# A two-layer scan network on one core: the second layer's side work cut into lagged units, its decays moved to SBUF, half of its scan sources multiplied by VectorE

## The chip, the cores and the metric

The kernel runs on one core of a Trainium2 chip. Five engines work from their own in-order queues: TensorE (PE, with its weight loads as PEld), VectorE (DVE), ScalarE (ACT), GpSimd (POOL) and SyncE (SP), which issues nearly all DMAs. The metric is the device time of one execution in microseconds, the median of several.

## The reference, cut to what matters

Batch 2, 2048 tokens, width 256, all in float32. Layer 0 (a small state-space block and a mixture of experts) is left as it is. Layer 1, which is changed, is a bidirectional Mamba block with a feed-forward part and a second branch:

```
for d in (fw, bw):                       # bw runs over time backwards
    xi, z = split(LN(x) @ Win);  u = silu(conv4(xi))
    dt, B, C = ...u @ Wx...;     dt = softplus(dt @ Wdt + bdt)
    h[t] = exp(dt*A) * h[t-1] + (dt*u) * B[t]        # 512 channels x 16 states
    y = sum_n h[.., n] * C[n] + u * D
    out_d = (y * silu(z)) @ Wout
f  = LN(x + out_fw) + LN(x + out_bw)     # scaled and shifted
f  = LN(f + relu(f @ W1 + b1) @ W2 + b2) # feed-forward part
out = x1 + f + gelu(LN(x) @ Wup + bup) @ Wdn + ...   # butterfly matrices, folded to dense
```

## The kernel before, in words

Layer 1 works in 16 chunks ("steps" in the code): for each of two batches four forward chunks of 512 tokens, then four backward ones. A chunk has 512 channels (four groups `e` of 128 partitions) and 16 states `n`, so 64 scans of 128 x 512. The loop over `g` at L1100 goes through all 1024 scans of the layer; `k` is the scan's place in its chunk.

Half of the scans are of kind P, half of kind D (`kinds`, L755: the first eight scans of a chunk are D, then P and D alternate, and the last eight are P).

- A P scan: ACT writes the decay `exp(dt*A)` to SBUF (`a`, L806), four scans ahead. ACT scales the transposed `dt*u` by B (`bT`, L792), PE transposes it back into a PSUM bank (`ab`, L816), DVE scans `h<-a,ab` (L836), POOL copies the last column (`hn`, L844) and multiplies `h` by C (`g`, L845).
- A D scan: ACT writes the decay into a PSUM bank of the same ring `ab`, one scan ahead. POOL multiplies `dtu` by the broadcast row of B (`b`, L823), DVE scans in place in the bank, ACT copies the last column (L847), DVE multiplies by C (L848).

The ring `ab` has two banks, which decays of D scans and sources of P scans take in turn. Four scans later `collect` (L850) lets PE transpose each `g` into four accumulators `yacc` (L870). At a chunk's first scan it opens them with a matmul of zeros (L859) and adds the skip term (L863).

All other work of a chunk is a list of functions with guessed weights (`prepare_parts`, `finish_parts`, `ff_parts`, `late_parts`) that is popped between the scans, in proportion to `k`, as whole functions: `down` issues all 32 of its matmul records, `project_out` adds, takes statistics, waits for POOL's root and normalizes, at one place of the program. A forward chunk has only the projections of its neighbours beside its scans; a backward chunk has in addition the whole feed-forward part and the second branch for both of its halves. The tile framework's own scheduler may then reorder what stands in one engine's queue. Side work uses a second ring of two PSUM banks, `pp`.

`delta_u` (L733) makes `dtu` for the next chunk on POOL; `skip_term` (L748) scales `u` there.

Of the kernel before, what the change touches and what calls it, by code (L numbers as in the profile page):

```python
# [18 lines left out]
P = 128  # L19
B = 2  # L20
# [9 lines left out]
class Common:  # L30
# [36 lines left out]
    def stats(self, pool, src, n):  # L67

        nc = self.nc
        bs = pool.tile([P, n, 6], F32, tag="bs", name="bs", bufs=2)  # L70
        mv = pool.tile([P, n, 2], F32, tag="mv", name="mv", bufs=2)
        rs = pool.tile([P, n], F32, tag="rs", name="rs", bufs=2)
        for i in range(n):
            nc.vector.bn_stats(bs[:, i, :], src[:, i, :])
            nc.vector.bn_aggr(mv[:, i, :], bs[:, i, :])  # L75
        self.rstd(rs, mv[:, :, 1])
        return mv, rs
# [413 lines left out]
TB = T // P  # L491
NT = L // T


def layer1(tc, c, a, x1d, wupd, wdnd, bupd, out):
    nc = c.nc
    with ExitStack() as ctx:
# [9 lines left out]


# [5 lines left out]
        def prologue(b, k):  # L514
            xnT = ap.tile([P, 2, T], F32, tag="xnT", name="xnT", bufs=3)
            for h in range(2):
                r = 2 * k + h
                x1t = tp.tile([P, 2, D], F32, tag="x1t", name="x1t", bufs=2)
                nc.sync.dma_start(x1t, rows2(x1d[b], r))
                mv, rs = c.stats(tp, x1t, 2)  # L520
                xn = tp.tile([P, 2, D], F32, tag="xn", name="xn", bufs=2)
                c.normalize(xn, x1t, mv, rs, 2)
                nc.sync.dma_start(rows2(xn1d[b], r), xn)
                ps = c.pp()
                for kk in range(2):
                    for i in range(2):
                        nc.tensor.transpose(
                            ps[:, kk * 256 + i * P : kk * 256 + (i + 1) * P],
                            xn[:, i, kk * P : (kk + 1) * P],
                            c.ident,  # L530
                        )
                nc.scalar.copy(
                    xnT[:, :, h * 256 : (h + 1) * 256], ps.rearrange("p (k t) -> p k t", k=2)
                )
            nc.sync.dma_start(xnTd[b][k], xnT)
            return xnT
# [39 lines left out]
        zero = wp.tile([P, P], F32, name="zero")  # L576
        nc.gpsimd.memset(zero, 0.0)
        ident4 = c.ident.unsqueeze(1).broadcast_to([P, 4, P])
# [68 lines left out]
        def gate(ck, zs, tb):  # L647

            ps = c.pp()
            for k in range(2):  # L650
                nc.tensor.matmul(
                    ps, ck.xnT[:, k, tb * P : (tb + 1) * P], ck.w["winz"][:, k, :],
                    start=(k == 0), stop=(k == 1),
                )
            nc.scalar.copy(zs[:, tb, :], ps)

        def conv(i, e):
# [5 lines left out]
            ps = c.pp()  # L663
            for k in range(2):
                nc.tensor.matmul(
                    ps, w["winx"][:, k, e * P : (e + 1) * P], ck.xnT[:, k, :],
                    start=(k == 0), stop=(k == 1),
                )
# [11 lines left out]
            for k in range(3):  # L680
                o = 3 - k if bw else k
                nc.vector.scalar_tensor_tensor(  # L682
                    ck.u[:, e] if k == 2 else ps, xi[:, o : o + T], pk[:, e, k : k + 1], ps,
                    ALU.mult, ALU.add,
                )
# [5 lines left out]

        def project(i):
            ck = steps[i]
            ps = c.pp()
            for e in range(4):
                nc.tensor.matmul(  # L696
                    ps, ck.w["wx"][:, e, :], ck.u[:, e, :], start=(e == 0), stop=(e == 3)
                )
# [5 lines left out]
        def rowsB(i):  # L704
            ck = steps[i]
            ps = c.pp()
            for tb in range(TB):
                nc.tensor.transpose(
                    ps[:, tb * P : (tb + 1) * P], ck.par[:, tb * P : (tb + 1) * P], c.ident
                )  # L710
            ck.BT = ap.tile([P, TB, NS], F32, tag="BT", name="BT")
            nc.scalar.copy(ck.BT, ps.rearrange("p (b m) -> p b m", b=TB)[:, :, 32:48])

        def delta(i, e):
# [6 lines left out]
            )  # L721
            nc.scalar.activation(
# [3 lines left out]
        def softplus(i):  # L726
            nc.scalar.activation(steps[i].dt, steps[i].dt, AF.Softplus)

        def delta_u(i, e):
# [3 lines left out]
            nc.gpsimd.tensor_mul(ck.dtu[:, e], ck.dt[:, e], ck.u[:, e])  # L733

        def delta_uT(i, tb):
# [8 lines left out]
            nc.scalar.copy(ck.dtuT[:, tb, :], ps)  # L744
# [10 lines left out]
        kinds = ["DD"] + ["PD"] * 6 + ["PP"]  # L755
# [9 lines left out]
        lo, hi = 0, 8  # L765
        for n in range(NS):
            ks = [k for k in range(K) if plan[k][1] == n and plan[k][3] == "P"]
            if ks:
                for q in range(TB):
                    fills[lo + q * (hi - lo) // TB].append((n, q))  # L770
                lo, hi = ks[0], ks[-1] + 1
# [25 lines left out]
        def decay(g):  # L797
            i, k = divmod(g, K)
            ck = steps[i]
            m, n, e, kind = plan[k]  # L800
            r = R[g] = {}
            if kind == "P":
                r["a"] = sp.tile([P, T], F32, tag="a", name="a", bufs=5)
            else:
                r["a"] = r["ps"] = c.ab()
            nc.scalar.activation(r["a"], ck.dt[:, e], AF.Exp, scale=ck.w["A"][:, e, n : n + 1])  # L806

        def source(g):
# [3 lines left out]
            r = R[g]  # L812
            if kind == "P":
                r["b"] = r["ps"] = c.ab()
                for q in range(TB):
                    nc.tensor.transpose(  # L816
                        r["b"][:, q * P : (q + 1) * P],
                        ck.bT[n, q][:, e * P : (e + 1) * P],
                        c.ident,
                    )  # L820
            else:
                r["b"] = sp.tile([P, T], F32, tag="b", name="b", bufs=3)
                nc.gpsimd.tensor_mul(r["b"], ck.dtu[:, e], ck.bb[n])  # L823

        def scan(g):
# [6 lines left out]
            if kind == "P":  # L832
                h = sp.tile([P, T], F32, tag="h", name="h", bufs=4)
            else:
                h = r["ps"]
# [5 lines left out]
            gt = r["g"] = sp.tile([P, T], F32, tag="g", name="g", bufs=6)  # L841
            hn = ck.hn[:, e, n : n + 1]
            if kind == "P":
                nc.gpsimd.tensor_copy(hn, h[:, last : last + 1])  # L844
                nc.gpsimd.tensor_mul(gt, h, ck.cb[n])  # L845
            else:
                nc.scalar.copy(hn, h[:, last : last + 1])  # L847
                nc.vector.tensor_mul(gt, h, ck.cb[n])  # L848

        def collect(g):  # L850
# [3 lines left out]
            if k == 0:  # L854
# [3 lines left out]
                for tb in range(TB):  # L858
                    nc.tensor.matmul(  # L859
                        ck.y[tb], zero, ident4, start=True, stop=False, skip_group_check=True  # L860
                    )
                    for e2 in range(4):
                        nc.tensor.matmul(  # L863
                            ck.y[tb][:, e2 * P : (e2 + 1) * P],
                            ck.u[:, e2, tb * P : (tb + 1) * P], c.ident,
                            start=False, stop=False, is_transpose=True, skip_group_check=True,
                        )
            gt = R.pop(g)["g"]
            for tb in range(TB):
                nc.tensor.matmul(  # L870
                    ck.y[tb][:, e * P : (e + 1) * P], gt[:, tb * P : (tb + 1) * P], c.ident,
                    start=False, stop=(k == K - 1), is_transpose=True, skip_group_check=True,
# [9 lines left out]
        def turned(i, e):  # L882
# [8 lines left out]
            nc.scalar.copy(ck.ygT[:, e, :], ps)  # L891
# [4 lines left out]
        def project_out(i, h):  # L896
# [3 lines left out]
            xn = tp.tile([P, 2, D], F32, tag="xn", name="xn", bufs=2)  # L900
            nc.sync.dma_start(xn, rows2(xn1d[ck.b], r))
            if ck.bw:
                yf = tp.tile([P, 2, D], F32, tag="yf", name="yf", bufs=2)
                nc.sync.dma_start(yf, rows2(yfd[ck.b][ck.k], h))
            ps = c.pp()
            for n in range(2):
# [336 lines left out]
```

## Time and profile before

| | us |
|---|---|
| median of 3 runs | 4137.5 (4127.43 to 4138.06) |
| the profiled execution, its own time | 4139.88 |
| its span, first to last instruction | 4138.2 |
| first scan of layer 1 starts | 1647.0 |
| last scan of layer 1 starts | 4045.4 |
| a forward chunk in the middle (first `gated` to the next, 1913.0 to 2046.1) | 133.1 |
| a backward chunk (2496.2 to 2677.2) | 180.9 |
| mean granted TensorE clock, as a share | 0.794 |

Times in the profile are microseconds from the first instruction; "mean" is in nanoseconds. L836 is line 836 of the kernel before. `out<-in` names the tiles. A group's idle time is how long its engine stood still just before the instructions of the group, with what ended the wait. A DVE or POOL instruction's own duration can contain a wait, where it has started and is held: such time counts as busy.

### The profile page before, as it was taken

How to read it: one execution, taken by the hardware profiler on the slowest of the kernel's cores; microseconds unless marked ns; L12 is line 12 of the kernel's file. 1: busy time of each engine (PE TensorE's matmuls, PEld its weight loads, DVE VectorE, ACT ScalarE, POOL GpSimd, SP SyncE). 2: the span in 40 equal slices, each digit the busy share in tenths (PEclk: the TensorE clock that was granted, in tenths of full speed). 3: DMA queues.
4: the chain of work that ended last, by engine and by line, in shares of the span. 5: the costliest groups of instructions: out<-in, count | busy, mean ns of one | idle time of the engine just before them, and what ended most of it. 6: DMA issues, size and time to landing. Idle time of an engine off the chain costs nothing.

```text
span 4138.2 us, 41758 instructions
## 1 busy us (share of the span) xinstructions
PE 2927.6 (71%) x13136; PEld 2056.6 (50%) x13136; DVE 3327.6 (80%) x4436; ACT 2353.4 (57%) x4721; POOL 2038.9 (49%) x2197
## 2 busy tenths in 40 slices
PE   6445364657677666777777778787877778888887
PEld 3323242434444433455555656575655555656565
DVE  7899999887988975888888767777788888767782
ACT  3433434354655654766766665655666766665662
POOL 5465555200000002677776656655577776656661
PEclk8657565657676676888889989898988888889898
DMA  4322142312122124312212121212121212111110
GB/s 135 119 96 67 59 125 102 100 44 76 32 66 67 34 59 128 101 60 66 61 60 75 59 73 46 78 56 69 52 67 60 63 65 70 54 52 52 47 46 13
DMA packets 170995, 285.07 MB, mean 69 GB/s; under 512 B 18571, under 2 KB 90443, under 8 KB 165644
## 3 DMA queue, kind: packets, MB, share of 16 engines
q1 hardware_dynamic: 170166, 280.30, 22.7%
q8 instruction: 104, 1.70, 0.2%
q0 software_dynamic: 608, 2.10, 0.1%
q14 instruction: 117, 0.96, 0.1%
HBM read 240.66 MB, written 24.91 MB: 64 GB/s over the span
## 4 chain that ended last, share of the span: by engine, by line
DVE 21%; PE 16%; POOL 9%; ACT 8%; issue 6%; DMA 0%; DVEq 0%; SPq 0%; POOLq 0%; ACTq 0%
DVE h L836 6%; DVE ab L836 6%; POOL g L845 3%; DVE g L848 3%; PE pp L962 3%; PE yacc L870 2%; POOL b L823 2%; PE ab L816 2%; ACT ab L806 2%; PE pp L696 2%; DVE pp L682 2%; PE pp L909 1%; POOL dtu L733 1%; ACT zu L690 1%; PE pp L1007 1%
## 5 line engine op out<-in xcount | busy, mean ns | idle before, releaser
L823 POOL TENSOR_TENSOR b<-dtu,bb 128x512 f32<-128x512 f32 x512 | 651.8, 1278 | 280.1 <-DVE ab L836 262.6
L427 PE MATMUL yacc<-da,ident 128*128 128x256 f32 x1024 | 449.9, 585 | 475.5 <-DVE da L424 410.2
L870 PE MATMUL yacc<-ident,g 128*128 128x128 f32 x4096 | 676.4, 302 | 144.2 <-POOL g L845 104.4
L870 PEld LDWEIGHTS yacc<-ident,g 128*128 128x128 f32 x4096 | 534.7, 156 | 264.4 <-POOL g L845 144.9
L845 POOL TENSOR_TENSOR g<-h,cb 128x512 f32<-128x512 f32 x512 | 651.8, 1273 | 0.4 <-POOL hc L844 0.2
L836 DVE TENSOR_TENSOR_SCAN h<-a,hc,ab 128x512 f32<-128x512 f32 x384 | 483.4, 1268 | 164.4 <-PE ab L816 155.1
L427 PEld LDWEIGHTS yacc<-da,ident 128*128 128x128 f32 x1024 | 268.5, 286 | 638.7 <-ACT hc L421 168.9
L816 PE MATMUL ab<-ident,bT 128*128 128x128 f32 x2048 | 373.1, 308 | 261.3 <-DVE h L836 168.5
L836 DVE TENSOR_TENSOR_SCAN ab<-ab,hc,b 128x512 f32<-128x512 f32 x384 | 485.5, 1277 | 70.7 <-ACT ab L806 68.0
L806 ACT ACTIVATE ab<-dt,A 128x512 f32<-128x512 f32 x512 | 351.5, 690 | 222.5 <-DVE h L836 113.0
L816 PEld LDWEIGHTS ab<-ident,bT 128*128 128x128 f32 x2048 | 264.9, 156 | 415.5 <-DVE h L836 243.2
L806 ACT ACTIVATE a<-dt,A 128x512 f32<-128x512 f32 x512 | 365.9, 717 | 160.5 <-DVE h L836 160.3
L417 DVE TENSOR_TENSOR_SCAN h<-da,h,bt 128x256 f32<-128x256 f32 x512 | 437.3, 891 | 8.9 <-ACT h L415 7.4
L64 POOL TENSOR_SCALAR rs<-mv 128x2 f32<-128x2 f32 (+1 forms) x72 | 16.6, 231 | 827.0 <-DVE mv L75 823.8
L401 ACT ACTIVATE da<-dt,A 128x256 f32<-128x256 f32 x512 | 235.1, 500 | 271.7 <-PE yacc L427 271.1
L848 DVE TENSOR_TENSOR g<-ab,cb 128x512 f32<-128x512 f32 x512 | 341.3, 678 | 55.3 <-ACT hc L847 54.9
L792 ACT ACTIVATE bT<-dtuT,BT 128x512 f32<-128x512 f32 x512 | 359.9, 717 | 10.5 <-PE ab L816 10.4
L405 DVE SCALAR_TENSOR_TENSOR bt<-dt,small,bt 128x256 f32<-128x256 f32 x512 | 333.3, 658 | 11.0 <-ACT bt L402 10.1
L844 POOL COPY hc<-h 128x1 f32<-128x1 f32 x512 | 103.1, 201 | 450.0 <-DVE h L836 407.6
L107 POOL TENSOR_TENSOR bft<-bfy,bfw 128x512 f32<-128x512 f32 (+1 forms) x100 | 158.6, 1604 | 321.9 <-DMA bfw<-in_upc_dram 165.9
L402 ACT ACTIVATE bt<-da,nc,c 128x256 f32<-128x256 f32 x512 | 280.6, 589 | 0.0
L847 ACT COPY hc<-ab 128x1 f32<-128x1 f32 x512 | 80.1, 157 | 253.4 <-DVE ab L836 251.1
(201 smaller groups left out, 5634.5 us busy)
## 6 DMA issues: line engine op xcount, KB each, us to landing
cb<-bcd SPq DMA_DIRECT2D x256, 256.0 KB
cb<-cd SPq DMA_DIRECT2D x128, 256.0 KB
bb<-bcd SPq DMA_DIRECT2D x128, 256.0 KB
bfw<-in_upc_dram SPq DMA_DIRECT2D x20, 1024.0 KB
bfw<-in_dnc_dram SPq DMA_DIRECT2D x20, 1024.0 KB
relay<-inter SPq DMA_DIRECT2D x128, 128.0 KB
f1c<-in_f_dram SPq DMA_DIRECT2D x8, 1024.0 KB
f2bd<-in_f_dram SPq DMA_DIRECT2D x16, 512.0 KB
```

The costliest lines, as they stand in the source:

```text
L402: nc.scalar.activation(bt[:, j], da[:, j], AF.Identity, scale=c1[:, e, s], bias=nc1[:, e, s])
L405: nc.vector.scalar_tensor_tensor(bt[:, j], dt[:, e], small[:, e, s], bt[:, j], ALU.mult, ALU.add)
L417: nc.vector.tensor_tensor_scan(h[:, j, 1 : LC + 1], da[:, j], bt[:, j], h[:, j, 0:1], ALU.mult, ALU.add,)
L427: nc.tensor.matmul(ys[e][:, 0:LC], c.ident, da[:, j], start=(n == 0), stop=(n == NS - 1))
L792: nc.scalar.activation(t, ck.dtuT[:, q, :], AF.Copy, scale=ck.BT[:, q, n : n + 1])
L806: nc.scalar.activation(r["a"], ck.dt[:, e], AF.Exp, scale=ck.w["A"][:, e, n : n + 1])
L816: nc.tensor.transpose(r["b"][:, q * P : (q + 1) * P], ck.bT[n, q][:, e * P : (e + 1) * P], c.ident,)
L823: nc.gpsimd.tensor_mul(r["b"], ck.dtu[:, e], ck.bb[n])
L836: nc.vector.tensor_tensor_scan(h[:, step], r["a"][:, step], r["b"][:, step], 0.0 if ck.first else steps[i - 1].hn[:, e, n : n + 1], ALU.mu ...
L845: nc.gpsimd.tensor_mul(gt, h, ck.cb[n])
L848: nc.vector.tensor_mul(gt, h, ck.cb[n])
L870: nc.tensor.matmul(ck.y[tb][:, e * P : (e + 1) * P], gt[:, tb * P : (tb + 1) * P], c.ident, start=False, stop=(k == K - 1), is_transpose=T ...
```

## The change

Only layer 1 changes (and `stats`, which is split into `moments` and the root).

1. **Scans.** All decays go to SBUF, six scans ahead (`AHEAD`, eight buffers instead of five). A D scan's source is multiplied by DVE straight into the `ab` bank that it then scans, so that PE (P) and DVE (D) alone write that ring. All scans write `h` to SBUF; POOL takes the last column and the multiply by C for all 64 (it had both for 32, and the source of the other 32). `collect` follows three scans later instead of four, and `g` has five buffers instead of six.
2. **Accumulators.** The zero matmuls go; the first transpose opens the bank, and the skip term is added later (`skip_term`, `skip_add`).
3. **Side work as units.** Each function is cut into units `U` of about two matmuls, each with followers that come a set number of scans later (`EV`, `DV`, `PO`, `PE`): a PE unit, then its copy out by ACT, then DVE, then the root on POOL, then DVE. `merged` interleaves several lists with at most two open `pp` banks, and `spread` stretches them over the chunk's scans. SiLU, softplus and GELU have fixed places (`SILU`, `SOFT`, `GELU`).
4. **Where the feed-forward work goes.** The second branch (`network_parts`) runs one half in every chunk, forward chunks too, and leaves `x1p` in DRAM. The rest (`ff_parts`) follows a chunk or more later (`FEEDS`), and reads `yd` and `x1p` back from DRAM.
5. **Moves between engines.** `delta_u` from POOL to DVE; two adds (`shift`, `last`) from DVE to POOL; the copies of the last column of D scans from ACT to POOL.
6. **Order.** Inside `tc.manual_schedule` the four compute engines keep the order in which the program is written. The prologue's `xnT` is read back from DRAM.

The core of the diff:

```diff
-        kinds = ["DD"] + ["PD"] * 6 + ["PP"]
+        kinds = ["DD", "PD", "PD", "PD", "PD", "PD", "PD", "PP"]
...
-            if kind == "P":
-                r["a"] = sp.tile([P, T], F32, tag="a", name="a", bufs=5)
-            else:
-                r["a"] = r["ps"] = c.ab()
+            assert ck.dt_made
+            r["a"] = sp.tile([P, T], F32, tag="a", name="a", bufs=AHEAD + 2)
             nc.scalar.activation(r["a"], ck.dt[:, e], AF.Exp, scale=ck.w["A"][:, e, n : n + 1])
...
-            else:
-                r["b"] = sp.tile([P, T], F32, tag="b", name="b", bufs=3)
-                nc.gpsimd.tensor_mul(r["b"], ck.dtu[:, e], ck.bb[n])
...
+            if kind == "D":
+                r["b"] = c.ab()
+                nc.vector.tensor_mul(r["b"], ck.dtu[:, e], ck.bb[n])
+            h = sp.tile([P, T], F32, tag="h", name="h", bufs=4)
             nc.vector.tensor_tensor_scan(
...
-            if kind == "P":
-                nc.gpsimd.tensor_copy(hn, h[:, last : last + 1])
-                nc.gpsimd.tensor_mul(gt, h, ck.cb[n])
-            else:
-                nc.scalar.copy(hn, h[:, last : last + 1])
-                nc.vector.tensor_mul(gt, h, ck.cb[n])
+            gt = r["g"] = sp.tile([P, T], F32, tag="g", name="g", bufs=5)
+            nc.gpsimd.tensor_copy(ck.hn[:, e, n : n + 1], h[:, last : last + 1])
+            nc.gpsimd.tensor_mul(gt, h, ck.cb[n])
...
-                for tb in range(TB):
-                    nc.tensor.matmul(
-                        ck.y[tb], zero, ident4, start=True, stop=False, skip_group_check=True
-                    )
...
-            nc.gpsimd.tensor_mul(ck.dtu[:, e], ck.dt[:, e], ck.u[:, e])
+            nc.vector.tensor_mul(ck.dtu[:, e], ck.dt[:, e], ck.u[:, e])
...
+EV, DV, PO, PE, LAG = 1.2, 1.2, 0.6, 1.2, 1.5
+AHEAD = 6
+FF_AT = 22
+BEHIND = 3
+LATE = 56
+SILU, SOFT, GELU = 32, 48, 14
...
+            us[3].then, us[3].closes = ((DV, norm), (PO, root), (DV, store), (PO, shift)), 0
...
+        with tc.manual_schedule(engines={nc.tensor.engine, nc.scalar.engine, nc.vector.engine, nc.gpsimd.engine}):
+            for g in range(-AHEAD, N + BEHIND):
+                if 0 <= g < N:
+                    i, k = divmod(g, K)
+                    if k == 0:
+                        todo = merged([early_parts(i)], 0, 1.0)[1]
+                        todo += spread(chains(i), BEHIND + 1.2, K - 0.5)
+                        todo.sort(key=lambda x: x[0])
+                    if k % 8 == 0 and k + 8 < K:
+                        load_bc(i, k // 8 + 1)
+                if 0 <= g + AHEAD < N:
+                    decay(g + AHEAD)
+                if 0 <= g < N:
+                    for n, q in fills[k]:
+                        scaled(i, n, q)
+                if 0 <= g + 1 < N:
+                    source(g + 1)
+                if 0 <= g < N:
+                    scan(g)
+                if 0 <= g - BEHIND < N:
+                    collect(g - BEHIND)
+                if 0 <= g < N:
+                    while todo and (todo[0][0] < k + 1 or k == K - 1):
+                        todo.pop(0)[2]()
```

## The prediction

> **What bounds the kernel now.** I read the page's engine totals first (DVE 80%), then the windows of layer 1, because an 80% over the whole span says nothing of the stage that is changed. The columns after the length are PE, PEld, DVE, ACT and POOL busy, the granted clock, and DMA:
>
> ```profile
> 1647.00:4047.00 2400.00, 1893.13 (x9723) 1391.72 (x9721) 1894.22 (x2232) 1565.90 (x2771) 1578.31 (x1914) 0.89 0.21 63
> 1904.00:2037.00 133.00, 101.79 (x524) 71.58 (x524) 113.44 (x127) 90.08 (x161) 95.04 (x117) 0.86 0.22 67
> 2487.00:2668.00 181.00, 146.63 (x734) 110.35 (x732) 129.35 (x164) 110.96 (x194) 105.27 (x130) 0.91 0.22 64
> ```
>
> The scans of layer 1 take 2400 us, 150.0 per chunk: 133 in a forward chunk, 181 in a backward one. DVE is busy for 118.4 of the 150 (1894.22/16), and in no chunk is any engine full. So the layer is paced by hand-overs. Who holds DVE up, from the waits of that stretch (total, times, longest):
>
> ```profile
> DVE h L836 <- PE ab L816: 202.2, 130, 9.1
> DVE ab L836 <- ACT ab L806: 89.5, 118, 4.9
> DVE g L848 <- ACT hc L847: 54.9, 131, 1.9
> DVE xn L82 <- POOL rs L65: 49.2, 40, 1.8
> DVE x1t L966 <- PE pp L962: 32.2, 12, 3.0
> DVE yf L82 <- POOL rs L65: 25.2, 14, 2.4
> ```
>
> P scans wait for their transposes, D scans for a decay that comes only one scan ahead, the multiply by C for ACT's copy, normalizing for POOL's root. Why the transposes are late is in PE's timeline of a backward chunk (start, duration):
>
> ```profile
> 2357.79 7.17 PE L962 MATMUL pp<-wdn,gff 128*128 128x256 f32 x32 [1.11 <-ACT hc L847]
> 2364.80 0.60 PE L816 MATMUL ab<-ident,bT 128*128 128x128 f32 x4
> ```
>
> One block of side work holds PE's queue for 7.2 us, and the sources of the next scans stand behind it. The same rows give PE's true pace: (7.17-0.4)/31 = 0.22 us per 256-column record, (0.60-0.27)/3 = 0.11 per transpose.
>
> **The change part by part**, per chunk of 64 scans. Consecutive instructions overlap a little, so I use start-to-start times where the timeline has them: a multiply on DVE 0.60 (two L880 take 1.26), a scan 1.19, a multiply on POOL 1.22 (four L733 take 4.95), its column copy 0.14.
>
> *DVE.* A D scan loses its multiply by C (678 ns, L848) and gains its source; the nearest row with two SBUF inputs is L919 at 683 ns, so nothing. The output in PSUM is bounded by L848 from PSUM and L682 at 736: at most 2 us, below nothing by the 8 ns to L1015 (670), taken as 0. delta_u comes in, 4 x 0.60 = +2.4; two adds per chunk leave, -1.2. DVE: 119.6.
>
> *POOL.* 98.6 now (1578.31/16). Less 32 sources (39.0) and 4 delta_u (4.9), plus 32 multiplies by C with copies (43.5), plus two adds (2.4): 100.6.
>
> *ACT.* 97.9 now, less 32 copies of 157 ns: 93. The table switches stay in number; SiLU with two loads is 1.28+3.62+1.28 = 6.2 us, which today stalls D scans whose decay is one ahead. Six decays ahead are some 12 us: hidden. Without that cover it would be up to 4 us at each of three places.
>
> *PE.* The zero matmuls go (83.8 us busy in all, off the path except at a chunk's head, where they wait for L880). What stays, by counts over 16: about 440 transposes x 0.11, 128 records of 256 columns x 0.22, 48 of 512 x 0.43 = 97 us at full clock, 109 at 0.89. It hides beside DVE, but at 84% of a 130 us chunk, not loosely: units of about 0.9 us between 0.44 us transposes.
>
> *The price that today's scans don't pay.* Every DVE instruction of the scan loop has one SBUF tensor and one in PSUM, and L836 never exceeds 1294 ns beside a busy POOL. The new source multiply reads two SBUF tensors. Layer 0 shows what that meets, POOL and DVE in one stretch:
>
> ```profile
> 312.58 3.35 POOL L107 TENSOR_TENSOR bft<-bfy,bfw 128x512 f32<-128x512 f32 x2 [2.24 <-DMA bfw<-in_upc_dram]
> 316.01 2.67 POOL L108 TENSOR_TENSOR bfy<-bfy,bfw 128x1024 f32<-128x1024 f32 x1
> ...
> 313.11 1.69 DVE L408 TENSOR_TENSOR bt<-bt,u 128x512 f32<-128x512 f32 x1
> ...
> 316.40 2.83 DVE L417 TENSOR_TENSOR_SCAN h<-da,h,bt 128x256 f32<-128x256 f32 x1
> ```
>
> L408 takes 1.69 instead of 0.68 us; it is held until POOL's instruction ends. Two POOL multiplies take 3.43 start to start instead of 2.44: each DVE instruction costs POOL some 0.5 (0.32 at 254 us). The Trainium skill speaks against this change here: "SBUF — State Buffer", section "SBUF: two separate sides", says that a DVE instruction with two SBUF inputs and a GpSimd one that reads SBUF take a port pair exclusively, whole instruction by whole instruction. By that rule POOL and the 39 such DVE instructions of a chunk (32 sources, 4 delta_u, 3 others) need 100.6 + 39 x 0.60 = 124 us; by the rows, at 0.45 each, 118. I take 118: the rows show part of the handover hidden.
>
> Walking a P-D pair with these numbers: DVE needs 1.19+0.60+1.19 = 2.98, POOL 2.72 + 0.45 = 3.17. POOL is the slower, works without pause, and the source multiply arrives about 0.2 us before the end of a POOL instruction: 24 x 0.2 = 5 us of waiting per chunk. If DVE's other work throws the phase off, the wait is up to 1.22 and 0.6 on average, 19 us.
>
> *Waits that go.* D's decay, ACT's copy, and most root and pp waits. The source's bank is free when the P scan two places before ends, about 1.8 us before it is needed, and PE needs 0.9: a unit in the way can still make it late. Today these waits are 202.2/16 = 12.6 us per chunk; without the 7 us blocks I put 5, between 0 and 15. What is late next is POOL, through the four `h` buffers.
>
> *Order and buffers.* In written order a `collect` that waits for POOL holds the next source on PE. It comes three scans (6 us) after its scan, and POOL needs 1.4 us per scan, so it waits only where POOL trails by three scans; four `h` buffers stop DVE near there anyway: 0, and inside PE's rival if not. Five `g` buffers for three scans of delay, and the eight `bT` filled one state ahead, are the same answer. DVE's and ACT's followers come 1.2 scans (2.4 us) after their PE unit, which takes 0.9: 0, up to 1 us each where PE trails.
>
> *DMAs.* 64 transfers of 256 KB come in through `yd` and `x1p`, on SP's queue, past the broadcasts of B and C. DMA engines are 21% busy, and a broadcast has eight scans (16 us) until its use: 0, at most 2 us per chunk if SP waits on a late store. `fetch` precedes its use by four scans.
>
> *Ends.* The prologue's trip of `xnT` through DRAM: +5 us, between 2 and 8, no row shows it alone. After the last scan 91.5 us (4138.2-4046.7) become about 55: in the last chain each half loses up, GELU and down (from 4073.4 to 4095.5 and from 4103.8 to 4120.7), 39 us, and gains a trip through DRAM, partly overlapped.
>
> *Sum.* Per chunk 119.6 + 5 + 5 = 130. 1647 + 5 + 16 x 130 + 55 = 3787, plus 1.7 around the span: 3790, against 4139.9 of the profiled execution (0.06% above the median 4137.5, which I neglect).
>
> **The rivals.**
> *DVE almost alone.* The waits nearly vanish, 119 to 121 per chunk: 3612 to 3645. For it: DVE's extra work lets POOL catch up. Against: POOL with its handovers needs 118 too, and two full engines in step do not add up to one. 10%.
> *PE's queue.* Its 109 us in a fixed order: a transpose behind a `collect` that waits for POOL, behind a unit that waits for an ACT copy delayed by SiLU. At 138 to 148 per chunk: 3917 to 4077. For it: 202 us of waiting for L816 now. Against: those rows stand behind 7 us blocks. 17%.
> *Slower: each source multiply waits for a whole POOL instruction.* Layer 0's L408 waited 1.0 us. If POOL always trails by two scans and the phase never locks, 32 x 1.1 = 35 us, POOL's own share of it comes back as late `h` buffers, and with 5 from PE a chunk takes about 160: 4269. It decides from (4139-1709)/16 = 152 per chunk, that is, when a source waits 0.85 us on average beside those 5. Against: the walk gives 0.2, the random phase 0.6. 10%.
> *The units bunch after all* (the planner can't fit the chunk and piles units): as before in PE's queue, less the ACT and root waits; 145, 4029. 3%.
>
> **How the numbers follow.** Likeliest case, 122 to 137 per chunk: 60%, 3660 to 3900. With the rivals above that is 60 + 10 + 17 + 10 + 3. The range from 3640 to 3990 leaves out most of the first rival, half of PE's and the slower one. A measurement of this kernel can tell 0.3% (12 us) from no change: faster 0.88, same 0.01, slower 0.11 (the slower rival and a PE queue worse than sized).
>
> **What would show it.** Right: forward and backward chunks equally long, near 130; DVE over 90% busy in them, the source row on DVE longer than 0.68 us and POOL's g row longer than 1.27; no waits for ACT's decays; L816's successor under 80 us of DVE waiting in all. Wrong: the source row near 1.7 us (the slower rival), DVE waiting over 200 us for `ab` from PE (PE's queue), the source and g rows at 0.68 and 1.27 (no port cost), or blocks of 7 us still in PE's timeline.

## The result, and the profile after

4082.5 us, the median of four runs (4073.7 to 4085.4), against 4137.8 before on the same chip: a ratio of 0.9868 with an interval of 0.9846 to 0.9891. The change makes the kernel 1.3% faster, 55 us, where about 350 were forecast (3790); 4082 lies above the range given (3640 to 3990). The profiled execution took 4085.35 (span 4083.6), so it stands for the median.

The page's totals after the change, and then the windows of layer 1, read as those in the prediction (length, then PE, PEld, DVE, ACT, POOL busy, granted clock, DMA). The first row is all scans, the second a forward chunk, the third a backward one:

```profile
PE 2816.0 (69%) x13008; PEld 2028.0 (50%) x13008; DVE 3513.6 (86%) x4468; ACT 2298.8 (56%) x4211; POOL 2283.9 (56%) x2676
```

```profile
1658.00:4023.70 2365.70, 1818.49 (x9737) 1389.91 (x9738) 2076.95 (x2250) 1522.09 (x2279) 1827.16 (x2396) 0.88 0.22 69
1929.00:2069.00 140.00, 107.89 (x580) 81.74 (x580) 125.04 (x132) 94.49 (x139) 109.52 (x145) 0.89 0.21 67
2513.00:2673.00 160.00, 119.79 (x624) 90.04 (x624) 139.31 (x156) 97.52 (x146) 116.57 (x156) 0.87 0.25 77
```

Divide the first row by 16: a chunk takes 147.9 us (150.0 before), of which DVE is busy for 129.8 (118.4 before) and idle for 18.0 (31.6 before). Nearly as much work came onto DVE as waiting left it. Chunks are more even than before (140 and 160 here, 133 and 181 then), and the time after the last scan fell from 91.5 to 59.9 (4083.6-4023.7).

DVE's main waits beside the scans (total, times, longest):

```profile
DVE h L937 <- PE ab L922: 128.4, 111, 9.0
DVE xn L86 <- POOL rs L65: 31.2, 27, 1.5
DVE h L937 <- ACT gff L1068: 18.6, 4, 5.6
DVE h L937 <- ACT dt L827: 14.3, 14, 1.4
```

The waits for D's decay and for ACT's copy (89.5 and 54.9) are gone. The wait for the transposes went from 202.2 only to 128.4. The rows that make DVE busier, by form, DVE's scans, and POOL's rows (count, busy us and mean ns, idle before):

```profile
L935 DVE TENSOR_TENSOR ab<-dtu,bb 128x512 f32<-128x512 f32 x512 | 427.9, 836 | 10.7
L839 DVE TENSOR_TENSOR dtu<-dt,zu 128x512 f32<-128x512 f32 x64 | 46.4, 745 | 1.0 <-ACT dt L832 1.0
L937 DVE TENSOR_TENSOR_SCAN h<-a,hc,ab 128x512 f32<-128x512 f32 x768 | 965.7, 1273 | 178.5 <-PE ab L922 91.6 <-ACT gff L1068 18.6 <-ACT dt L827 11.7
L937 DVE TENSOR_TENSOR_SCAN h<-a,ab 128x512 f32<-128x512 f32 x256 | 306.3, 1214 | 58.9 <-PE ab L922 36.7 <-ACT dt L827 2.6 <-PE yacc L956 1.7
L944 POOL TENSOR_TENSOR g<-h,cb 128x512 f32<-128x512 f32 x1024 | 1313.6, 1283 | 0.6 <-POOL hc L943 0.6
L943 POOL COPY hc<-h 128x1 f32<-128x1 f32 x1024 | 370.9, 362 | 510.0 <-DVE h L937 476.8 <-DMA cb<-bcd 8.9 <-PE yacc L956 5.5
```

The source takes 836 ns where the multiply by C that it replaces took 678: (836-678) x 32 = 5.1 us per chunk. The mean hides a wide spread, as the shortest, the median and the longest source show (ns):

```profile
L935 DVE TENSOR_TENSOR ab<-dtu,bb x512: 666/700/1853, 1655.7 to 4004.5; 128x512 f32<-128x512 f32 x171
```

Half of the sources take 700 ns or less, others up to 1.85 us. The price is seen in the two engines' timelines (start, duration) of one stretch:

```profile
2001.38 0.80 DVE L935 TENSOR_TENSOR ab<-dtu,bb 128x512 f32<-128x512 f32 x1
2002.28 2.45 DVE L937 TENSOR_TENSOR_SCAN h<-a,hc,ab 128x512 f32<-128x512 f32 x2
```

```profile
2000.34 1.28 POOL L944 TENSOR_TENSOR g<-h,cb 128x512 f32<-128x512 f32 x1
2001.56 0.65 POOL L943 COPY hc<-h 128x1 f32<-128x1 f32 x1
2002.17 1.27 POOL L944 TENSOR_TENSOR g<-h,cb 128x512 f32<-128x512 f32 x1
2003.62 0.18 POOL L943 COPY hc<-h 128x1 f32<-128x1 f32 x1 [0.18 <-DVE h L937]
```

DVE's source starts at 2001.38, while POOL's multiply runs to 2001.62 (2000.34 + 1.28), and takes 0.80 us, 0.1 more than the median. POOL's next instruction, a copy of one column, then takes 0.65 us and ends with the source, where a copy beside a scan takes 0.18. In this stretch the two engines are in step, as the prediction's walk had them. What remains of PE's side is in its timeline of a backward chunk:

```profile
2541.53 1.02 PE L713 MATMUL pp<-winz,xnT 128*128 128x512 f32 x2
2546.76 2.07 PE L713 MATMUL pp<-winz,xnT 128*128 128x512 f32 x2 [4.21 <-DVE xn L1016]
2548.62 1.06 PE L922 MATMUL ab<-ident,bT 128*128 128x128 f32 x4
```

The blocks of 7 us are gone, but a unit (L713) waits 4.21 us for a bank of `pp` that DVE's add has to free, and the transposes of the next source stand behind it. In its turn that add stood on DVE behind a normalization that waited 1.46 us for POOL's root, and behind the four instructions after it, as DVE's timeline shows:

```profile
2540.87 1.80 DVE L86 TENSOR_SCALAR xn<-xn,mv,rs 128x256 f32<-128x256 f32 x2 [1.46 <-POOL rs L65]
2542.71 0.69 DVE L1029 TENSOR_TENSOR yf<-yf,xn 128x512 f32<-128x512 f32 x1
2543.43 0.69 DVE L1030 TENSOR_TENSOR yf<-yf,fwnw 128x512 f32<-128x512 f32 x1
2544.04 0.69 DVE L935 TENSOR_TENSOR ab<-dtu,bb 128x512 f32<-128x512 f32 x1
2544.84 1.28 DVE L937 TENSOR_TENSOR_SCAN h<-a,hc,ab 128x512 f32<-128x512 f32 x1
2546.04 0.66 DVE L1016 TENSOR_TENSOR xn<-xn,pp 128x512 f32<-128x512 f32 x1
```

### The profile page after: what moved, and what is told of

It is laid out like the page before. It is cut to its first block, busy times and chain, and to the rows that moved or that the text cites. A ratio compares the mean times of both kernels' runs of the same rounds, so it can differ in the third digit from the quotient of the medians.

```text
span 4083.6 us, 42541 instructions
## 1 busy us (share of the span) xinstructions
PE 2816.0 (69%) x13008; PEld 2028.0 (50%) x13008; DVE 3513.6 (86%) x4468; ACT 2298.8 (56%) x4211; POOL 2283.9 (56%) x2676
## 4 chain that ended last, share of the span: by engine, by line
POOL 15%; DVE 14%; PE 14%; issue 9%; ACT 8%; DMA 1%; DVEq 0%; POOLq 0%; SPq 0%; ACTq 0%
POOL g L944 9%; DVE h L937 6%; POOL hc L943 3%; PE yacc L956 3%; PE pp L1059 2%; DVE ab L935 2%; ACT a L913 2%; PE ab L922 2%; PE pp L1083 1%; ACT bT L901 1%; POOL zu L857 1%; PE pp L713 1%; PE pp L819 1%; PE pp L733 1%; DVE pp L762 1%
## 5 line engine op out<-in xcount | busy, mean ns | idle before, releaser
L944 POOL TENSOR_TENSOR g<-h,cb 128x512 f32<-128x512 f32 x1024 | 1313.6, 1283 | 0.6 <-POOL hc L943 0.6
L937 DVE TENSOR_TENSOR_SCAN h<-a,hc,ab 128x512 f32<-128x512 f32 x768 | 965.7, 1273 | 178.5 <-PE ab L922 91.6
L913 ACT ACTIVATE a<-dt,A 128x512 f32<-128x512 f32 x1024 | 727.7, 718 | 426.0 <-DVE h L937 424.9
L943 POOL COPY hc<-h 128x1 f32<-128x1 f32 x1024 | 370.9, 362 | 510.0 <-DVE h L937 476.8
L922 PE MATMUL ab<-ident,bT 128*128 128x128 f32 x2048 | 349.5, 298 | 139.4 <-DVE h L937 137.0
L935 DVE TENSOR_TENSOR ab<-dtu,bb 128x512 f32<-128x512 f32 x512 | 427.9, 836 | 10.7
L937 DVE TENSOR_TENSOR_SCAN h<-a,ab 128x512 f32<-128x512 f32 x256 | 306.3, 1214 | 58.9 <-PE ab L922 36.7
L428 DVE TENSOR_TENSOR da<-h,cb 128x512 f32<-128x512 f32 x256 | 221.3, 864 | 1.0
L733 PE MATMUL pp<-xnT,winx 128*128 128x512 f32 x256 | 155.8, 720 | 84.0 <-DVE zu L762 75.1
L412 DVE TENSOR_TENSOR bt<-bt,u 128x512 f32<-128x512 f32 x256 | 209.4, 818 | 1.2
```

Of the source, the lines that this page charges most:

```text
L922: nc.tensor.transpose(b[:, q * P : (q + 1) * P], ck.bT[n, q][:, e * P : (e + 1) * P], c.ident)
L935: nc.vector.tensor_mul(r["b"], ck.dtu[:, e], ck.bb[n])
L937: nc.vector.tensor_tensor_scan(h[:, step], r["a"][:, step], r["b"][:, step], 0.0 if ck.first else steps[i - 1].hn[:, e, n : n + 1], ALU.mu ...
L943: nc.gpsimd.tensor_copy(ck.hn[:, e, n : n + 1], h[:, last : last + 1])
```

## The experiments

The theory after the result (A): the small units of side work bring what a loosened PE can bring, and the scan path takes most of it back, by the SBUF port pair that DVE's two-SBUF multiply and POOL share and by the multiply standing directly ahead of its own scan. The rivals (B and C): PE's queue in written order is the limit; or the written order is, or `delta_u` on DVE. All runs are medians of several executions; the kernel before took 4134 to 4140 beside them.

**e1, one SBUF input.** The source is made from B's broadcast alone (the multiply by `dtu` is left out); everything else is as after.

```diff
-                nc.vector.tensor_mul(r["b"], ck.dtu[:, e], ck.bb[n])
+                nc.vector.tensor_scalar(r["b"], ck.bb[n], 0.01, None, ALU.mult)
```

> The changed kernel, with the D source made from one SBUF tensor: DVE multiplies the broadcast row of B by a constant instead of by dtu, so this kernel leaves the factor dt*u out of half of the sources. Same number of DVE and POOL instructions, but no DVE instruction of the scan loop has two SBUF inputs. Theory A (DVE paces; port waits are one of three terms, some 5 us per chunk in the source and some more behind POOL's copies): the source row falls from 836 to about 690 ns, POOL's copy from 362 to about 200 ns, and the time by 80 to 130 us, to 3950 to 4000. Theory B (PE's queue paces): within 20 us of the changed kernel (4082). Theory C (POOL and the port pace): more than 200 us faster, under 3880.

Measured: 3987.2, ratio 0.9644 (0.9628 to 0.9661), 95 us under after. By form:

```profile
L935 DVE TENSOR_SCALAR ab<-bb 128x512 f32<-128x512 f32 x511 | 351.8, 688 | 10.7
L943 POOL COPY hc<-h 128x1 f32<-128x1 f32 x1023 | 210.4, 206 | 616.0 <-DVE h L937 575.5 <-DMA cb<-bcd 9.9 <-PE ab L922 8.6
```

Source 836 to 688 ns, copy 362 to 206; POOL's multiplies stay (1283 and 1284). Of the 95 us, 10 are an earlier first scan (1648 instead of 1658), which e2 shows too without this edit; the chunks give 85, or 5.3 each (147.9 to 142.5), 4.8 of it DVE's busy time. That is the price of the second SBUF operand in the changed kernel. Two other readings of this run fall away: the source also no longer waits for `dtu`, but DVE's idle time before it is 10.7 us in both; and a multiply with two SBUF inputs is not slow in itself (683 ns at L919 before).

**e2, the source one scan earlier.** The same multiply is issued in `source`, beside the P scans' transposes, so that a scan lies between it and its own.

```diff
+            else:
+                b = R[g]["b"] = c.ab()
+                nc.vector.tensor_mul(b, ck.dtu[:, e], ck.bb[n])
...
-            if kind == "D":
-                r["b"] = c.ab()
-                nc.vector.tensor_mul(r["b"], ck.dtu[:, e], ck.bb[n])
```

> The changed kernel, with the D source issued by DVE one scan earlier, before the scan of the P neighbour, so that the scan no longer stands directly behind the multiply whose bank it reads. Theory A: the multiply-to-scan step falls from 0.83 us (0.73 at its shortest) to about 0.60 us plus port waits, 4 us per chunk, 50 to 80 us in all: 4000 to 4030. Theories B and C: nothing, 4070 to 4095.

Measured: 4026.8, 0.9739 (0.972 to 0.9759), 56 us under after with the same computation. Per chunk DVE's busy time falls by 1.9 and its idle time by 1.3 (first row of after and this one, over 16). The idle time before scans that stands for no named engine goes from 60 us in all (237.4, of which 177.0 are for named ones) to 3 (200.3 and 197.5); waits for others, POOL's multiply above all (1.5 to 15.4 us), take a part of its place:

```profile
1648.10:3962.50 2314.40, 1793.02 (x9735) 1367.48 (x9734) 2047.21 (x2249) 1518.18 (x2278) 1827.29 (x2396) 0.90 0.24 70
```

**e3, a quarter of the P sources.** Only the first of four groups is transposed, and the others scan the same bank again; D scans share a bank likewise. It leaves out three of four P sources, 384 of the 512 sets of transposes.

```diff
-            if kind == "P":
-                b = R[g]["b"] = c.ab()
+            if kind == "P" and e == 0:
+                b = held["P"] = c.ab()
...
+            if kind == "P":
+                R[g]["b"] = held["P"]
```

> The changed kernel, with the P sources transposed by PE for the first of the four channel groups of a state only; the other three P scans read the same bank again, so this kernel leaves three quarters of the P sources out. D scans likewise keep one bank per state, still multiplied for every scan. DVE waits for PE at a quarter of the places. Theory A: the 128 us that DVE waits for ab from PE fall to under 40, and the time by 60 to 110 us: 3970 to 4020. Theory B: by more than 200 us, under 3880. Theory C: under 20 us.

Measured: 4037.7, 0.9766 (0.9748 to 0.9783), only 45 us under after, less than theory A had said. DVE still waits 90.3 us for `ab`, in 27 long waits instead of 111 short ones: 38 us of the 128.4 hang on the transposes' number. That the rest hangs on what stands ahead of them fits PE's timeline above, but this run doesn't show it by itself.

**e4, the scan path alone.** The kernel before, with the change's part 1, but for `collect`'s delay and the buffers of `g`, and nothing else (its functions between the scans, its scheduler, `delta_u` on POOL).

```diff
-        AHEAD = {"P": 4, "D": 1}
+        AHEAD = {"P": 6, "D": 6}
...
+            if kind == "D":
+                r["b"] = c.ab()
+                nc.vector.tensor_mul(r["b"], ck.dtu[:, e], ck.bb[n])
+            h = sp.tile([P, T], F32, tag="h", name="h", bufs=4)
```

> The kernel before, with part 1 of the change alone: all decays in SBUF six ahead, the D source by DVE into the bank, all h in SBUF, all multiplies by C and copies on POOL. Side work, its order and collect's delay stay as before. Theory A: the waits for ACT's decay and copy go (145 us), port waits and the dependent step come (5 + 4 us per chunk, 150 us): about no change, 4100 to 4180. Theory B: the 7 us blocks remain in PE's queue and nothing is gained, 4100 to 4160. If the gain of the whole change comes from this part, 4060 to 4100.

Measured: 4347.4, 1.0515 (1.0497 to 1.0532): 210 us slower than before, and more than either theory had given it.

**e5, the units alone, in written order.** The changed kernel with the old scan path.

```diff
+                r["d"] = sp.tile([P, T], F32, tag="b", name="b", bufs=3)
+                nc.gpsimd.tensor_mul(r["d"], ck.dtu[:, e], ck.bb[n])
...
+                nc.scalar.copy(ck.hn[:, e, n : n + 1], h[:, last : last + 1])
+                nc.vector.tensor_mul(gt, h, ck.cb[n])
```

> The changed kernel with its units, lags, order and feed-forward placement, but with the scan path of before: P decays four ahead in SBUF, D decays one ahead in the ab bank, D sources multiplied by POOL, D scans in place, copy by ACT and multiply by C on DVE from the bank. The first theory (a scan part that is neutral, a units part that gives the gain) expects about the changed kernel's time, 4040 to 4120. After the scan part alone took 4347, theory D says that the scan part costs some 50 to 200 us in any surroundings and the units save all: 3880 to 4030. The opposite, that the units live from the early decays and are worthless without them (written order, ACT's SiLU ahead of a decay that is needed at once): over 4150.

Measured: 4149.1, 1.0024 (1.0015 to 1.0033): no gain, 67 us over after, at the edge of the case that the units are worthless without the early decays. DVE's waits say why:

```profile
DVE g L955 <- ACT hc L954: 231.2, 503, 5.1
DVE ab L944 <- ACT ab L916: 96.2, 59, 6.1
```

In written order every multiply by C comes directly behind its scan, with ACT's copy from the same bank between them in the program.

**e6, the change without the written order.** `if True:` in place of `with tc.manual_schedule(...):`.

> The changed kernel without the fixed order: the framework's scheduler may reorder each engine's queue again. If the written order with its lags is what keeps PE and DVE in step, 60 to 200 us slower, 4140 to 4280. If the order is neutral, within 20 us of 4082. If the written order makes PE stand behind held pp banks (the 180 us that PE waits with a source behind it), faster: 4000 to 4060.

Measured: 4092.8, 0.989 (0.9875 to 0.9905), 10 us over after: for the new scan path the order is nearly neutral, as one of the three cases had it.

**e9, the units alone, order free.** e5 with the same edit as e6.

> The units with the scan path of before, and with the framework's scheduler free to reorder each queue. In e5 the written order put every D multiply by C directly behind its scan and ACT's copy, and DVE stood 227 us for that copy. If the units are worth something without the early decays, as soon as DVE may put another scan in between: 3980 to 4080. If the units and the scan path only work together: 4110 to 4200.

Measured: 3955.0, 0.956 (0.9541 to 0.9579): the fastest version that computes everything, 127 us under the changed kernel, and better than its best case. The scans' windows of e9 and e6:

```profile
1647.80:3884.30 2236.50, 1800.07 (x9732) 1336.41 (x9732) 1928.69 (x2254) 1579.01 (x2792) 1558.82 (x1882) 0.92 0.23 73
```

```profile
1657.70:4030.90 2373.20, 1848.56 (x9728) 1376.03 (x9728) 2057.39 (x2247) 1533.74 (x2277) 1807.45 (x2388) 0.89 0.22 69
```

Per chunk DVE is busy for 120.5 in e9 and 128.6 in e6; idle for 19.2 and 19.7. All of the difference of 8.5 us but 0.5 is DVE's busy time, and the rows by form account for it: e9's multiply by C, then e6's source.

```profile
L955 DVE TENSOR_TENSOR g<-ab,cb 128x512 f32<-128x512 f32 x512 | 340.8, 676 | 53.5 <-ACT hc L954 41.4 <-POOL g L952 7.2 <-issue 3.3
```

```profile
L935 DVE TENSOR_TENSOR ab<-dtu,bb 128x512 f32<-128x512 f32 x512 | 468.2, 921 | 9.1
```

(468.2-340.8)/16 = 8.0 us.

**e7, e1 to e3 together.** It leaves out what e1 and e3 leave out.

> The three cuts at once: the D source from one SBUF tensor (leaves out dt*u there), issued one scan earlier, and only a quarter of the P sources transposed (leaves out the rest). Alone they took 95, 56 and 45 us from 4082. If they are separate terms of DVE's queue (theory A) they add up: 196 us, 3870 to 3910. If they are one and the same slack counted three times: 3950 to 3990. If one hides another, less than 3860.

Measured: 3911.2, 0.9446 (0.9428 to 0.9464), 171 us under after; the three alone add up to 196. The costs are largely separate (25 us are counted twice), and with all three gone a chunk still takes 137.2, not 130.

**e8, `delta_u` back on POOL.** One word in `delta_u`, `nc.gpsimd` for `nc.vector`.

> The changed kernel with delta_u back on POOL, where it was before. DVE loses 2.8 us per chunk (four multiplies of 0.60 to 0.75 us), POOL gains 5. Theory A (DVE paces, POOL has 29 us per chunk of idle time): 30 to 50 us faster, 4035 to 4055. Theory C (POOL and the port pace): 60 to 90 us slower.

Measured: 4116.6, 0.9947 (0.9932 to 0.9962), 34 us over after, against both theories (A had it faster, C slower by 60 to 90): that move is a gain. DVE's waits for roots grow, which fits roots that stand behind four multiplies in a row on POOL (`DVE y L86 <- POOL rs L65` is 36.5 us, 3.6 in after).

**e10 and e11, more P scans**, both on e2, so that PE makes more of the sources:

```diff
-        kinds = ["DD", "PD", "PD", "PD", "PD", "PD", "PD", "PP"]
+        kinds = ["DD", "PD", "PD", "PD", "PD", "PP", "PP", "PP"]   # e10
+        kinds = ["DD"] + ["PP"] * 7                                # e11
```

> The source issued ahead (e2), and in two of the six mixed groups of eight scans both states of kind P: 40 P and 24 D scans per chunk instead of 32 and 32. DVE loses eight source multiplies of 0.86 us per chunk (6.9 us), ACT gains eight of 0.61, PE 32 transposes of 0.11 (3.5 us). Theory A (DVE paces, the source's port wait included): 70 to 110 us less than e2's 4027, 3920 to 3960. If PE's window for a P source between two P scans (1.19 us) is too short: 4000 to 4060.

> As e10, with all scans after the first eight of a chunk of kind P: 56 P and 8 D. DVE loses 24 sources (20.6 us per chunk), ACT gains 14.7 and stands at about 110 us per chunk, PE gains 10.5 and stands at 107 at full clock, 120 at the granted 0.88. Theory A alone, without another engine in the way: 3700. With PE's window for each source only one scan long and its queue in written order, PE paces: 3900 to 4150, and DVE waits over 300 us for ab.

Measured: 4068.3 (0.9833, 0.981 to 0.9855) and 4078.5 (0.9859, 0.9837 to 0.9882); e2 had 4026.8. Both are slower than e2; e10 lies above both of its cases, e11 where PE was said to pace. DVE's wait for `ab` in e10, then in e11:

```profile
DVE h L937 <- PE ab L922: 235.3, 189, 10.0
```

```profile
DVE h L937 <- PE ab L922: 416.7, 356, 8.9
```

DVE's busy time falls to 109.6 per chunk in e11, but its idle time rises to 38.3 (18.0 in after). In e11 PE's queue is the bound; already the eight more P scans of e10 cost more waiting than they save.

**e12, more room between `pp` banks.** The planner counts a bank as free 1.0 scans after its last reader (`free.append(at + 1.0)`) instead of 0.01.

> The changed kernel with one number of the planner changed: a pp bank counts as free one scan after its last reader is placed, instead of at once, so that PE's units open later and stand less behind held banks. If P sources are late because PE stands behind banks that DVE's convolution taps still hold (70+77 and 44+48 us of waiting), those waits halve and DVE's 128 us for ab fall to under 70: 4020 to 4055. If the bunching that the tighter plan brings (units up to two per scan) costs as much: 4070 to 4110.

Measured: 4077.3, 0.9859 (0.984 to 0.9877), 5 us under after, within the noise of the two. DVE's wait for `ab` is 119.3 us in 65 waits (128.4 in 111), where under 70 would have spoken for the banks. This doesn't settle how much of PE's lateness comes through those banks.

**e13, e6 with e1's edit**, and **e14, e4 with e1's edit**: what is the port's in each setting (both leave out the multiply by `dtu` in the D scans' source).

> Left to the scheduler (e6, 4093) instead of the written order, and the D scans' source computed from the broadcast of B alone (times a constant instead of delta_u), so that it reads one SBUF tensor; the output is not the reference's. The same units with the old scan path took 3955 (e9), so the scan path costs 138 us in this order. Theory A (that cost is the port pair that DVE's two-SBUF multiply and POOL share): nearly all of it goes, 3955 to 3990. Theory B (the port is a part of it, as in e1 where it gave 95; the rest is the order of dependent instructions: multiply ahead of its own scan, all h buffers and columns through POOL): 3990 to 4030.

> The kernel before with the scan path alone (e4, 4347, 210 us slower than before), and the D scans' source from the broadcast of B alone, one SBUF tensor; the output is not the reference's. Theory A (port): the loss is the port's, 4140 to 4200. Theory B (with the 7 us blocks still on PE, POOL's doubled output work lags, and h buffers and the root come late whatever the port does): 4230 to 4320.

Measured: 3956.9 (0.9561, 0.9538 to 0.9585) and 4209.4 (1.017, 1.0155 to 1.0185). e13 equals e9: with the scheduler free, the whole loss of the scan path, 138 us against 136, goes with that one operand. In e14 138 of 210 us go, and 72 stay (4209 lies just above theory A's 4200). The windows of e4 and e14:

```profile
1639.70:4249.70 2610.00, 1953.15 (x9742) 1420.80 (x9741) 2015.43 (x2231) 1523.61 (x2263) 1845.12 (x2430) 0.85 0.19 58
```

```profile
1634.80:4118.00 2483.20, 1929.09 (x9744) 1401.97 (x9744) 1895.20 (x2230) 1520.31 (x2264) 1658.72 (x2432) 0.86 0.19 60
```

DVE's busy time goes from 126.0 to 118.5 per chunk, which is that of before; its idle time stays at 37 (before: 31.6), and 16 x 5.2 = 83 us is about what stays. DVE waits there for `zu` of POOL (5.4 us before), whose queue now holds every scan's output work beside whole blocks of side work:

```profile
DVE h L830 <- POOL zu L748: 89.1, 12, 8.0
```

**e15 and e16, the copy behind the multiply**: e5 and e9 with these two lines exchanged.

```diff
-                nc.scalar.copy(ck.hn[:, e, n : n + 1], h[:, last : last + 1])
                 nc.vector.tensor_mul(gt, h, ck.cb[n])
+                nc.scalar.copy(ck.hn[:, e, n : n + 1], h[:, last : last + 1])
```

> The units in the written order with the old scan path (e5, 4149), with the D scan's multiply by C written ahead of ACT's copy of its last column instead of behind it. In e5 the multiply stood behind that copy 486 times, 227 us. Theory A (that hand-over is what the written order costs the old path, 194 us against e9): 3950 to 4000. Theory B (the copy moves behind the multiply and holds the bank, so the next decay comes later by as much): 4080 to 4150.

> The fastest so far (e9, 3955: units, old scan path, scheduler free), with the same swap. Theory A (the 41 us of waits for ACT's copy go): 3915 to 3950. Theory B (the scheduler had filled most of that gap with other work, and the copy now ends later and holds the bank of the next decay, which DVE already awaits for 55 us): 3955 to 3990.

Measured: 4208.4 (1.0166, 1.0149 to 1.0183) and 3977.2 (0.9609, 0.9595 to 0.9623): 59 and 22 us slower than e5 and e9, against theory A in both, and in e15 worse than theory B's 4150 too. In e15 the wait only moved, to the decay that needs the bank:

```profile
DVE ab L944 <- ACT ab L916: 282.1, 159, 6.9
```

The runs that matter, as one table (medians in us):

| side work | old scan path | new scan path | new, source with one SBUF input |
|---|---|---|---|
| functions, scheduler | 4138 (before) | 4347 (e4) | 4209 (e14) |
| units, scheduler | **3955 (e9)** | 4093 (e6) | 3957 (e13) |
| units, written order | 4149 (e5) | 4083 (after) | 3987 (e1) |

Down a column one reads what the units and the order bring, along a row what the scan path costs and what of it is the port. The units, with parts 2, 4 and 5 of the change, which no run separates from them, bring 183 us. The new scan path takes 138 of them back. The written order is worth 10 for the new path, and costs the old one 194: it puts a scan, ACT's copy and the multiply by C directly behind one another, and DVE's wait for that copy is 231.2 us in e5 and 41.4 in e9. The new path has no such step.

## Why the prediction was wrong in size

The sign held, and so did several steps. The terms that were mis-sized lie between the 130 us forecast for a chunk and the 147.9 measured. With the ends, 16 x 17.9 + 6 + 5 = 297 us, the forecast's 3787 becomes 4084; the span is 4083.6.

- **"DVE: 119.6"**: right for the units. e9, which has the same moves of `delta_u` and the adds, and the old scan path, is busy for 120.5.
- **"without the 7 us blocks I put 5" (waits that go): the first failing step.** After the change DVE idles for 18.0 per chunk, 13 more than that, 208 us in all. From the waits of after: 128.4/16 = 8.0 are for the transposes (5 forecast), about 2 for POOL's root and 2.6 for ACT, which I took to vanish, and some 5 stand for no named engine. The transposes' part is not the new scan path's doing: DVE waits 123.9 us for them in e9, 119.7 in e6 and 104.9 in e13. Small units took away the long block, but a transpose still stands behind whatever unit is late, as the one that waited 4.21 us for its `pp` bank.
- **The step from a source to its scan, put at 0.60 us: a term taken at nothing.** That is the step of two multiplies that don't depend on each other; the source stands directly ahead of the scan that reads it. In e1, whose sources pay no price at the port, one takes 688 ns and about 60 us are idle before the 512 scans behind them (233.5 before all scans, 173.0 of it for named engines): the step is 0.81, so by estimate 0.21 x 32 = 6.7 us per chunk. In after 60/16 = 3.8 of it is idle time, most of the 5 us above, and the rest is overlap that is lost, counted as busy. e2 puts a scan between, this idle time goes, and of the 6.7 us it wins 3.2.
- **"A D scan loses its multiply by C and gains its source; so nothing", with 5 us of waiting for the port: right in size, but not all.** DVE is busy for 129.8, where 119.6 + 5 had been put: 5.2 us per chunk over, 83 in all. The source row alone is 5.1 over the multiply it replaces, as forecast. What is over is, as far as the rows show, the lost overlap just named, `delta_u` at 745 ns and the final multiply (L1177) at 1233, which have two SBUF inputs too, and smaller rows. In free order the source takes 921 ns, and the price is 8 us.
- **The rule and the rows.** By the prediction's estimate from the rule of the Trainium skill ("SBUF — State Buffer", section "SBUF: two separate sides") POOL needed 124 us per chunk, by the rows of layer 0 118. Measured: POOL is busy for 1827.16/16 = 114.2, against 102.1 in e1 (1633.66/16), where 100.6 had been put without the price. e1 changes 32 of the 39 DVE instructions, so each of them costs POOL 12.1/32 = 0.38 us, and DVE 0.15 (836 against 688): under both. The rule was right on whom it hits: e1 and e13 change one operand and move 95 and 136 us. That a shared port is the reason comes from that rule; the runs show what the operand costs, and a copy that ends with the source beside it.
- **"24 x 0.2"**: right at the mean, by luck in part. A source takes 0.15 us more than in e1 at the mean, but not 0.2 each: the median is 700 ns, next to e1's 695, and the longest 1853. The two engines are in step in some stretches only. The slower rival (1.1 us each) is out, as is a random phase (0.6).
- **POOL as the next limit**: not seen. DVE's waits for `g` stayed at 1.5 us in all (15.4 in e2, where DVE is held up less).
- **ACT's waits**: those for the decay and the copy went, as stated. But in e9, where they stay, they are 96.5 us (55.1 and 41.4), and the scan path that removes them costs 138.
- **Ends**: 1658 for the first scan where 1652 was put, 59.9 after the last where 55 was: nearly right. The start is not constant (1634.8 to 1658.0 in these runs).
- **Even chunks near 130**: half right. The difference fell from 48 to 20 us; backward chunks still have more units in them.
- **The tests.** The source row, the missing ACT waits, and the missing blocks came out as stated. POOL's `g` row was longer than 1.27 us, as stated, but by 10 ns (1283), and it is 1284 in e1 without the price: that sign told nothing, since the price fell on the copies. DVE at 88% (2076.95/2365.70), not over 90, and 128.4 us of waits for `ab`, not under 80, told against the likeliest case. The result is nearest to the rival of PE's queue (138 to 148), for which 17% had been given; but it is PE's queue, the price of the second SBUF operand, and the step from source to scan together: in e3 three quarters of the P sources go, and with them only 45 us.

Left open: what makes the last 1.3 us per chunk of idle time without a named engine, why waits for POOL's root and for ACT stayed, and what the `pp` banks cost by themselves (e12 didn't tell).

## What to carry to other kernels

Judge each half of a combined change by itself, and against the other's best setting: here the half meant to take waits away cost 138 of the 183 us that the other half won. When an operation moves between engines, count how many of its operands lie in SBUF while a second engine works there; a source made from two SBUF tensors was no like-for-like trade for a product with one in PSUM. And don't book a wait as gone because its longest cause goes: scale it by what the queue still has ahead of it, since DVE's idle time stayed at 15 to 20 us per chunk in after, e1, e2, e6, e7, e9 and e13. And where an instruction stands directly ahead of the one that reads its result, don't use the step of independent ones.

## What the runs showed of the hardware that was not expected

- Most of the port's price on POOL was paid by its smallest instruction. The copy of one column, 128x1, took 362 ns on average beside the two-SBUF sources and 206 without them (e1), 0.65 us where it met one; the 128x512 multiplies next to it stayed at 1283 ns.
- A DVE instruction with one SBUF input and its output in PSUM was not slowed by a busy POOL: 688 ns at the mean, 696 at the longest of 512 (e1).
- A DVE scan that reads what the multiply just before it wrote starts 0.72 to 0.90 us after it (1992.67 to 1993.39 and 2001.38 to 2002.28 in DVE's timeline after), where two independent multiplies (L880 before) followed each other at 0.60. In e1, where the source is not held, it is 0.81 at the mean.
- In the written order the source met POOL at a better moment than in the scheduler's: 836 against 921 ns at the mean, 700 against 828 at the median.
